# Planner steps per scan and delayed TensorE sums in the last chunks of an attention and Mamba kernel

## The chip, the cores and the metric

The kernel runs on one core of one Trainium2 chip. The time is that of the device, in microseconds (us), the median of several executions. The engines are named as in the profile: PE is TensorE (PEld its weight loads), DVE is VectorE, ACT is ScalarE, POOL is GpSimd, and SP issues the loads and stores of this kernel. Each engine works through its own queue in the order in which the program issued it.

## What is computed

Two layers follow each other, on four images of 128 channels and 64 x 64 pixels, in f32. The first is attention over the 4096 pixels of an image (four heads of 32), with an output projection, a residual and a layer norm. The second is the sum of three things: a 3 x 3 convolution, a spectral part (a 1 x 1 convolution on the Fourier transform), and a Mamba block. Only the last matters here:

```python
xi, z = split(in_proj(u))                  # 256 inner channels each
xs = silu(causal_conv1d(xi, 4 taps))
dt, Bm, Cm = split(x_proj(xs))             # dt through dt_proj and softplus
h[n]  = exp(dt * A[n]) * h[n] + dt * Bm[n] * xs      # 16 states n, along the pixels
y     = sum over n of h[n] * Cm[n], + xs * D
out   = out_proj(y * silu(z))
```

## The kernel before

The pixels are cut into 32 chunks of 512 (eight per image). A chunk's 256 inner channels are two halves of 128 partitions, so a chunk has 2 x 16 = 32 states, each a row of work on 128 x 512 elements:

- ACT computes the decay `dA = exp(dt * A)` into PSUM (`scan_decay`, L813), for which there are two PSUM tiles in the tail.
- DVE in the tail, POOL before it, computes the input term `db = u * B` (`scan_input_term`, L818).
- DVE runs the recurrence (`scan_state`, L829), called the scan of a state below.
- POOL copies the last column into `state` (L838, left out in the last chunk of an image) and multiplies by C in place (L839).
- The product is added to the chunk's sum: by POOL into an SBUF tile (L856 and L858) for all chunks but the last two. For chunks 30 and 31 it is added by PE, with an identity matrix as weights, into a PSUM tile (L851 for the first term, L852 for the states). There the scan writes into one of four tiles of V that attention no longer needs.

B and C of a state pair are broadcast from DRAM to all partitions by two rows of a load on SP (L796 into one of three ring buffers, L802 into tiles of K or V that attention has left, which the list `spare` hands out). A state pair needs 512 KB.

One Python loop writes all instructions out in a fixed order; nothing is reordered afterwards. Its counter t advances by one for each block of keys of the attention (32 blocks, 64 chunk and head-pair combinations: t from 0 to 2047) and runs on to 2239. A chunk's states take 64 steps, one state on every even step; the scan of chunk c begins at step 144 + 64 c. So when attention ends, chunk 29 still has its states 24 to 31 to scan, and chunks 30 and 31 come after it, at steps 2064 and 2128. This last part, from t = 2049, is called the tail. On an even step the loop issues the scan, the copy, the multiplication and the addition of a state; on an odd step the decay of the next state, the input term of the one after it, and a load.

Everything else is written as generators, "jobs", that a `Plan` advances: the projections, the layer norm, the input of the next chunk's scan (`mamba_input`, `scan_input`, `scan_bc`, `scan_dt`), `spectral`, `convolve` (nine taps and a tenth matmul, L903 and L908), the gate `silu(z)` of a chunk (`gate`), `scan_output` (gate, out_proj, sum), and `flips` (the last sum of the chunks whose mirrored rows come late). A job yields what its next piece needs: "P", "D" and "A" are places on PE, DVE and ACT, "B" is one of two PSUM banks, "f" the right to the one output tile, and an empty string only the next step. `plan.step` is called once in every t and gives each job, in order of rank, at most one advance if there are places left; only PE pieces may follow each other in the same call. In the tail each call has four places of each of the three engines. `sigmoid`, used by the gate and by `scan_input`, yields five such pieces: ACT abs (L615), ACT exp (L617), ACT ln into a bank (L620), DVE combination (L623), ACT exp (L625).

Between the scan of a state and the next in DVE's queue stand the input term and whatever jobs have put there; between two decays on ACT, likewise; between the additions of two states on PE, likewise. In `scan_state` the addition on PE is issued right after POOL's multiplication, in the same step.

Of the kernel before, what the change touches and what calls it, by code (L numbers as in the profile page):

```python
# [9 lines left out]
F32 = mybir.dt.float32  # L10
F32R = mybir.dt.float32r
AF = mybir.ActivationFunctionType
ALU = mybir.AluOpType
# [4 lines left out]
P = 128  # L18
# [5 lines left out]
L = 512  # L24
# [3 lines left out]
NH = DI // P  # L28
NS = 16
# [52 lines left out]
class Job:  # L82
# [4 lines left out]
    def __init__(self, gen):  # L87
        self.gen = gen
        self.done = False
        self.need = None  # L90
        self.advance(None)
# [8 lines left out]
class Plan:  # L100


    def __init__(self, banks, buffers):
        self.t = None
        self.places = buffers
        self.seq = 0
        self.later = []
        self.jobs = []
        self.free = list(range(banks))
        self.freed = []  # L110
# [11 lines left out]
    def step(self, t, places):  # L122

        self.t = t
        self.places |= places
        self.free += [bank for when, bank in self.freed if when <= t]
        self.freed = [e for e in self.freed if e[0] > t]
        for e in sorted((e for e in self.later if e[0] <= t), key=lambda e: e[:3]):
            self.jobs.append((e[1], e[0], e[2], Job(e[3])))
            self.later.remove(e)  # L130
        self.jobs = sorted((j for j in self.jobs if not j[3].done), key=lambda j: j[:3])
        kept = 0
        for *_, job in self.jobs:
            bank = None
            if "B" in job.need and len(self.free) <= kept:
                continue
            if any(c != "B" and not self.places[c] for c in job.need):
                kept += "B" in job.need
                continue
            for c in job.need:  # L140
                if c == "B":
                    bank = self.free.pop(0)
                else:
                    self.places[c] -= 1
            job.advance(bank)
            while not job.done and job.need == "P" and self.places["P"]:
                self.places["P"] -= 1
                job.advance(None)
        self.jobs = [j for j in self.jobs if not j[3].done]

# [5 lines left out]
def attention_then_conv_mamba(  # L156
# [17 lines left out]
    nc = tc.nc  # L174
# [3 lines left out]
    NT = N // P  # L178
    CHUNKS = B * NCH
    HALVES = CHUNKS * PAIRS  # L180
# [4 lines left out]
    loc = ctx.enter_context(tc.tile_pool(name="loc", bufs=2))  # L185
    dram = ctx.enter_context(tc.tile_pool(name="dram", bufs=2, space=DRAM))
    psum = ctx.enter_context(tc.tile_pool(name="psum", bufs=1, space=PSUM))
# [12 lines left out]
    for h in range(HEADS):  # L200
        k, j = divmod(h, 2)
        c = COL["bk"] + k
# [8 lines left out]
    for h in range(HEADS):  # L211
        k, j = divmod(h, 2)
        c = COL["bq"] + h
# [33 lines left out]
    ident = cst[:, K_ID : K_ID + P]  # L247
# [64 lines left out]
    plan = Plan(2, {"x": 2, "f": 1})  # L312
# [315 lines left out]
    xps, xss, dts, us, accs, gates, xds, bcds = ({} for _ in range(8))  # L628
# [154 lines left out]
    spare = [((HALVES - 1) * NT + 1, KK[0][i : i + 2]) for i in range(0, NCH, 2)]  # L783
    spare += [(HALVES * NT + 12, KK[1][i : i + 2]) for i in range(0, NCH, 2)]
    spare += [(HALVES * NT + 20, VA[i : i + 2]) for i in range(4, NCH, 2)]
    taken, ring = {}, [3]
# [33 lines left out]
    def scan_state(c, v):  # L820

        n, hf = divmod(v, NH)
        k = hf * NS + n
        assert (c, hf) in scaled
        if c >= CHUNKS - 2:
            hs = flat(VA[v % 4])
        else:
            hs = loc.tile([P, L], F32, tag="hs", name=f"hs_{c}_{k}")
        nc.vector.tensor_tensor_scan(  # L829
            hs,  # L830
            dA.pop((c, v)),
            db.pop((c, v)),
            state[:, k : k + 1] if c % NCH else zero,
            ALU.mult,
            ALU.add,
        )
        if c % NCH < NCH - 1:
            nc.gpsimd.tensor_copy(state[:, k : k + 1], hs[:, L - 1 :])  # L838
        nc.gpsimd.tensor_tensor(hs, hs, bcs[c, n][1], ALU.mult)  # L839
        if hf == NH - 1 and (c, n) in taken:  # L840
            spare.append((plan.t + 6, taken.pop((c, n))))
        elif hf == NH - 1:
            ring[0] += 1
        if c >= CHUNKS - 2:

            if v == 0:
                late = psum.tile([P, NH, L], F32, tag=f"s{CHUNKS - c}", name=f"acc_{c}")
                for h in range(NH):
                    accs[c, h] = late[:, h, :]
            if n == 0:  # L850
                nc.tensor.matmul(accs[c, hf], ident, xss[c][hf], start=True, stop=False)  # L851
            nc.tensor.matmul(accs[c, hf], ident, hs, start=False, stop=n == NS - 1)  # L852
        elif n == 0:
            acc = loc.tile([P, L], F32, tag=f"acc{hf}", name=f"acc_{c}_{hf}")
            accs[c, hf] = acc
            nc.gpsimd.tensor_tensor(acc, xss[c][hf], hs, ALU.add)  # L856
        else:
            nc.gpsimd.tensor_tensor(accs[c, hf], accs[c, hf], hs, ALU.add)  # L858

    hxs, yms, edges, wd, ymd = {}, {}, set(), {}, {}  # L860

# [74 lines left out]
    def scan_output(c):  # L936

        b, i = divmod(c, NCH)
        late = i < NCH // 2
        yield "f"  # L940
        while not all(gates[c]) or c not in yms:
            yield ""

        for hf in range(NH):
            if c >= CHUNKS - 2:
                acc = loc.tile([P, L], F32, tag=f"acc{hf}", name=f"acc_{c}_{hf}")
                nc.vector.tensor_tensor(acc, accs[c, hf], gates[c][hf], ALU.mult)
                accs[c, hf] = acc
            else:
                nc.gpsimd.tensor_tensor(accs[c, hf], accs[c, hf], gates[c][hf], ALU.mult)  # L950
        if not late:
            wr = load_flipped(c)
        for _ in range(3):
            yield ""
        bank = yield "PB"
        pf = bank_tile(bank, [P, L], f"py1_{c}")
        for hf in range(NH):
            if hf:
                yield "P"
            nc.tensor.matmul(  # L960
                pf, outw[:, hf, :], accs[c, hf], start=hf == 0, stop=hf == NH - 1
            )
        yield "D"
        plan.release(bank, 2)
        ob = loc.tile([P, L], F32, tag="ob", name=f"ob_{c}", bufs=1)
        nc.vector.tensor_tensor(ob, yms.pop(c), pf, ALU.add)
        if late:
            yield ""
            ymd[c] = dram.tile([P, L], F32, tag="ymd", name=f"ymd_{c}", bufs=NCH)
            nc.sync.dma_start(ymd[c], ob)  # L970
        else:
            add_flipped(ob, wr)
            yield ""
            yield ""
            nc.sync.dma_start(out[b, :, i * L : (i + 1) * L], ob)
        plan.places["f"] += 1
# [20 lines left out]
    LEAD = 7  # L997
    SLOT = PAIRS * NT
    LAG = 2 * SLOT + 16
# [19 lines left out]
    for c in range(CHUNKS):  # L1019
        t0 = (c + 1) * SLOT  # L1020
        plan.at(t0, 0, load_residual(c))
        plan.at(t0 + 16, 1, mamba_input(c))
        plan.at(t0 + SLOT + 30, 3, convolve(c))
        plan.at(c * SLOT + LAG + 6, 3, gate(c))
        plan.at((c + 1) * SLOT + LAG + 2, 0, scan_output(c))
    for b in range(B):
        for i in range(NCH // 2):
            plan.at((b + 1) * NCH * SLOT + 44 + 10 * i, 4, flips(b * NCH + NCH // 2 - 1 - i))
# [1 line left out]
    t = 6 - SLOT  # L1030
    loaded = 0
    end = (CHUNKS + 3) * SLOT
    while t < end or not plan.idle():
        H, m = divmod(t, NT)
        if 0 <= H < HALVES:
            scores_for_exp(H, m)
        h1, s1 = divmod(t + LEAD, NT)
        if 0 <= h1 + 1 < HALVES:
            scores_for_max(h1 + 1, s1)
        H, m = divmod(t - 1, NT)  # L1040
        last = m == NT - 1
        if last and 0 <= H < HALVES:
            times_values(H, m)
        c, s = divmod(t - LAG, SLOT)
        odd = s % 2 == 1
        if -1 <= c < CHUNKS:
            v = c * STATES + s // 2
            if not odd:
                if v >= 0:
                    scan_state(*divmod(v, STATES))  # L1050
            else:
                if 0 <= v + 1 < CHUNKS * STATES:
                    scan_decay(*divmod(v + 1, STATES))
                if 0 <= v + 2 < CHUNKS * STATES:
                    late = t > HALVES * NT
                    scan_input_term(
                        *divmod(v + 2, STATES), nc.vector if late else nc.gpsimd
                    )

                if loaded < CHUNKS * NS and loaded // NS in bcds:  # L1060
                    if ring[0] or spare[0][0] <= t:
                        scan_load(*divmod(loaded, NS))
                        loaded += 1
        if t < -LEAD or t > HALVES * NT:
            plan.step(t, {"D": 4, "P": 4, "A": 4})
        elif odd:
            plan.step(t, {"D": 2, "P": 2, "A": 2})
        else:
            plan.step(t, {"D": 0, "P": 0, "A": 1})
        if not last and 0 <= H < HALVES:  # L1070
            times_values(H, m)
        t += 1
# [76 lines left out]
```

## Time and profile before

| | us |
|---|---|
| median of 3 runs | 6135.8 (6135.27 to 6138.95) |
| the profiled execution, its own time | 6136.61 |
| its span | 6134.7 |
| attention's last matmul ends about | 5891 |
| scan of state 0 of chunk 30 starts | 5923.6 |
| scan of state 0 of chunk 31 starts | 6042.7 |
| last scan starts | 6122.8 |

Over the whole span PE is busy for 5914.9 us (96%), DVE for 4291.6, ACT for 3557.2 and POOL for 4534.8. These are averages over a long attention stage and a short tail; the tail has to be read for itself. In the tables of stretches a line gives start and end, length, and then the busy time of each engine with its number of instructions. In the order of time a line gives start, duration, engine, source line, operation, output and inputs, and in brackets how long the engine stood idle before it and what ended the wait. In the list of waits a line gives who waited for whom, the total, the number of times and the longest. In names, V and K are attention's tiles, in the tail used for the scan's results and for B and C.

### The profile page before, as it was taken

How to read it: one execution, taken by the hardware profiler on the slowest of the kernel's cores; microseconds unless marked ns; L12 is line 12 of the kernel's file. 1: busy time of each engine (PE TensorE's matmuls, PEld its weight loads, DVE VectorE, ACT ScalarE, POOL GpSimd, SP SyncE). 2: the span in 40 equal slices, each digit the busy share in tenths (PEclk: the TensorE clock that was granted, in tenths of full speed). 3: DMA queues.
4: the chain of work that ended last, by engine and by line, in shares of the span. 5: the costliest groups of instructions: out<-in, count | busy, mean ns of one | idle time of the engine just before them, and what ended most of it. 6: DMA issues, size and time to landing. Idle time of an engine off the chain costs nothing. (4 is left out here: it accounts for less than half of the span.)

```text
span 6134.7 us, 82692 instructions
## 1 busy us (share of the span) xinstructions
PE 5914.9 (96%) x31434; PEld 2454.4 (40%) x31434; DVE 4291.6 (70%) x4404; ACT 3557.2 (58%) x4794; POOL 4534.8 (74%) x4785
## 2 busy tenths in 40 slices
PE   5999999999999999999999999999999999999966
PEld 2444444444444444444444444444444444444321
DVE  4556776777776777777767777677777677777647
ACT  1455666665666665666665666666565566566643
POOL 0006888778887777888877888877888787788877
PEclk7999999999999999999999999999999999999988
DMA  4012222224322222222332322222432222222222
GB/s 126 23 35 57 75 65 73 72 69 110 89 78 74 72 70 71 73 66 84 102 89 72 74 75 65 73 72 68 111 82 75 69 65 63 65 66 69 67 82 82
DMA packets 265503, 455.21 MB, mean 74 GB/s; under 512 B 45577, under 2 KB 47121, under 8 KB 265105
## 3 DMA queue, kind: packets, MB, share of 16 engines
q1 hardware_dynamic: 261584, 448.11, 26.9%
q8 instruction: 246, 4.03, 0.3%
q10 hardware_dynamic: 3520, 1.82, 0.1%
q14 instruction: 153, 1.25, 0.1%
HBM read 375.63 MB, written 65.80 MB: 72 GB/s over the span
## 5 line engine op out<-in xcount | busy, mean ns | idle before, releaser
L446 DVE TENSOR_REDUCE part<-s 128x2 f32<-128x1024 f32 x2048 | 2497.4, 1220 | 1527.0 <-PE s L439 1526.5
L491 ACT ACTIVATE e<-s 128x1024 f32<-128x1024 f32 x2048 | 2095.3, 1023 | 2203.1 <-PE s L483 2195.7
L503 PE MATMUL po<-e,V 128*33 128x512 f32 x8192 | 2158.6, 605 | 0.7
L483 PE MATMUL s<-Q,K 64*128 64x512 f32 x8192 | 1504.0, 445 | 7.1 <-ACT e L491 3.8
L439 PE MATMUL s<-K,Q 64*128 64x512 f32 x8192 | 1314.6, 398 | 31.5 <-DVE part L446 28.5
L839 POOL TENSOR_TENSOR hs<-hs,bc 128x512 f32<-128x512 f32 x952 | 1215.7, 1277 | 174.0 <-DVE hs L829 105.4
L483 PEld LDWEIGHTS s<-Q,K 64*128 64x128 f32 x8192 | 610.9, 185 | 1727.9 <-ACT e L491 1175.1
L818 POOL TENSOR_TENSOR db<-u,bc 128x512 f32<-128x512 f32 x948 | 1215.4, 1282 | 0.0
L858 POOL TENSOR_TENSOR acc<-acc,hs 128x512 f32<-128x512 f32 x900 | 1150.8, 1279 | 70.6
L829 DVE TENSOR_TENSOR_SCAN hs<-dA,state,db 128x512 f32<-128x512 f32 x832 | 1060.2, 1274 | 106.9 <-ACT dA L813 53.1
L439 PEld LDWEIGHTS s<-K,Q 64*128 64x128 f32 x8192 | 762.0, 185 | 255.2 <-DVE part L446 77.1
L483 PE MATMUL s<-MX,sel 64*128 64x512 f32 x4096 | 813.4, 394 | 25.9 <-DVE MX L470 25.9
L813 ACT ACTIVATE dA<-dt,negA 128x512 f32<-128x512 f32 x1024 | 703.1, 687 | 137.3 <-DVE hs L829 76.1
L838 POOL COPY state<-hs 128x1 f32<-128x1 f32 x864 | 159.9, 185 | 818.1 <-DVE hs L829 818.1
L503 PEld LDWEIGHTS po<-e,V 128*33 128x33 f32 x8192 | 299.8, 109 | 908.4 <-issue 894.1
L483 PEld LDWEIGHTS s<-MX,sel 64*128 64x128 f32 x4096 | 384.0, 184 | 129.2 <-DVE MX L470 38.6
L903 PE MATMUL pf<-xp,cw 128*128 128x512 f32 x576 | 288.5, 620 | 0.0
L455 POOL COPY wide<-mx 128x128 f32<-128x128 f32 x256 | 63.1, 290 | 202.5 <-DVE mx L452 202.5
L829 DVE TENSOR_TENSOR_SCAN hs<-dA,zero,db 128x512 f32<-128x512 f32 x128 | 163.0, 1274 | 1.5 <-POOL db L818 1.2
L852 PE MATMUL acc<-V,cst 128*128 128x512 f32 x128 | 92.4, 823 | 71.6 <-POOL V L839 71.2
L903 PEld LDWEIGHTS pf<-xp,cw 128*128 128x128 f32 x576 | 96.7, 188 | 135.4 <-issue 135.2
L701 POOL TENSOR_TENSOR xs<-xs,sg_x 128x512 f32<-128x512 f32 x64 | 82.4, 1287 | 59.1 <-ACT sg_x L625 59.1
(141 smaller groups left out, 3551.4 us busy)
## 6 DMA issues: line engine op xcount, KB each, us to landing
bc<-bcd SPq DMA_DIRECT2D x487, 512.0 KB
Q<-qd SPq DMA_DIRECT2D x256, 128.0 KB
K<-kd SPq DMA_DIRECT2D x64, 256.0 KB
K<-bcd SPq DMA_DIRECT2D x42, 256.0 KB
vd<-vst SPq DMA_DIRECT2D x32, 264.0 KB
V<-vd SPq DMA_DIRECT2D x32, 264.0 KB
xq<-in_x SPq DMA_DIRECT2D x32, 256.0 KB
xk<-in_x SPq DMA_DIRECT2D x32, 256.0 KB
```

The costliest lines, as they stand in the source:

```text
L439: nc.tensor.matmul(sc[:, j, :], QT[H][rows[j], n, t * P : (t + 1) * P], KK[k][m][rows[j], :], start=n == 0, stop=n == 1,)
L446: nc.vector.tensor_reduce(part[H][:, t, :, m], sc, AX.X, ALU.max)
L483: nc.tensor.matmul(s[:, j, :], sel[rows[j], :] if n == 2 else KK[k][i][rows[j], t * P : (t + 1) * P], mov[rows[j], :], start=n == 0, stop= ...
L491: nc.scalar.activation(e, s, AF.Exp)
L503: nc.tensor.matmul(po[H][used[j], :], VA[i][:, t, 2 * k + j, :], e[:, j, :], start=m == 0, stop=m == NT - 1,)
L813: nc.scalar.activation(dA[c, v], dts[c][hf], AF.Exp, scale=negA[:, k : k + 1])
L818: engine.tensor_tensor(db[c, v], us[c][hf], bcs[c, n][0], ALU.mult)
L829: nc.vector.tensor_tensor_scan(hs, dA.pop((c, v)), db.pop((c, v)), state[:, k : k + 1] if c % NCH else zero, ALU.mult, ALU.add,)
L838: nc.gpsimd.tensor_copy(state[:, k : k + 1], hs[:, L - 1 :])
L839: nc.gpsimd.tensor_tensor(hs, hs, bcs[c, n][1], ALU.mult)
L858: nc.gpsimd.tensor_tensor(accs[c, hf], accs[c, hf], hs, ALU.add)
L903: nc.tensor.matmul(pf, cw[:, k, :], xps[c][:, dy : dy + RPC, dx : dx + W], start=k == 0, stop=False)
```

## The change

In the tail (`plan.late`), four things differ.

- `plan.step` is called on odd steps only, so once for each scan and not twice, with four places on DVE and PE and six on ACT. Within one call a job now advances over as many "P", "A" and "D" pieces as follow each other, while there are places. It stops at an empty yield, at a bank, and at a need for two things at once.
- The addition of a state on PE is not issued with its scan, but kept in a list and issued two scans (four steps) later (`add_states`).
- From step 2052 on, the states of chunk 29 (26 to 31) are also summed by PE; its first 26 states stay in POOL's sum. `scan_output` then adds the two sums on DVE (two more instructions), and chunk 29's gate is multiplied on DVE and no longer on POOL.
- `scan_output` of chunks 29 to 31 becomes due four steps later. The test for a free load buffer also holds when `spare` is empty.

```diff
--- before.py
+++ after.py
@@ -102,6 +102,7 @@
 
     def __init__(self, banks, buffers):
         self.t = None
+        self.late = False
         self.places = buffers
         self.seq = 0
         self.later = []
@@ -143,8 +144,11 @@
                 else:
                     self.places[c] -= 1
             job.advance(bank)
-            while not job.done and job.need == "P" and self.places["P"]:
-                self.places["P"] -= 1
+
+            while not job.done and job.need in ("PAD" if self.late else "P"):
+                if not job.need or not self.places[job.need]:
+                    break
+                self.places[job.need] -= 1
                 job.advance(None)
         self.jobs = [j for j in self.jobs if not j[3].done]
 
@@ -822,7 +826,8 @@
         n, hf = divmod(v, NH)
         k = hf * NS + n
         assert (c, hf) in scaled
-        if c >= CHUNKS - 2:
+        late = plan.t > HALVES * NT + 1
+        if late:
             hs = flat(VA[v % 4])
         else:
             hs = loc.tile([P, L], F32, tag="hs", name=f"hs_{c}_{k}")
@@ -841,21 +846,31 @@
             spare.append((plan.t + 6, taken.pop((c, n))))
         elif hf == NH - 1:
             ring[0] += 1
-        if c >= CHUNKS - 2:
-
-            if v == 0:
-                late = psum.tile([P, NH, L], F32, tag=f"s{CHUNKS - c}", name=f"acc_{c}")
-                for h in range(NH):
-                    accs[c, h] = late[:, h, :]
-            if n == 0:
-                nc.tensor.matmul(accs[c, hf], ident, xss[c][hf], start=True, stop=False)
-            nc.tensor.matmul(accs[c, hf], ident, hs, start=False, stop=n == NS - 1)
+        if late:
+
+            if c not in sums_late:
+                sums_late[c] = psum.tile(
+                    [P, NH, L], F32, tag=f"s{1 + c % 2}", name=f"acc_{c}"
+                )
+            terms = [hs] if n else [xss[c][hf], hs]
+            for x in terms:
+                waiting.append((plan.t + 4, c, hf, x, n == NS - 1 and x is hs))
         elif n == 0:
             acc = loc.tile([P, L], F32, tag=f"acc{hf}", name=f"acc_{c}_{hf}")
             accs[c, hf] = acc
             nc.gpsimd.tensor_tensor(acc, xss[c][hf], hs, ALU.add)
         else:
             nc.gpsimd.tensor_tensor(accs[c, hf], accs[c, hf], hs, ALU.add)
+
+    sums_late, waiting, begun = {}, [], set()
+
+    def add_states():
+        while waiting and waiting[0][0] <= plan.t:
+            _, c, hf, x, last = waiting.pop(0)
+            nc.tensor.matmul(
+                sums_late[c][:, hf, :], ident, x, start=(c, hf) not in begun, stop=last
+            )
+            begun.add((c, hf))
 
     hxs, yms, edges, wd, ymd = {}, {}, set(), {}, {}
 
@@ -942,10 +957,14 @@
             yield ""
 
         for hf in range(NH):
-            if c >= CHUNKS - 2:
-                acc = loc.tile([P, L], F32, tag=f"acc{hf}", name=f"acc_{c}_{hf}")
-                nc.vector.tensor_tensor(acc, accs[c, hf], gates[c][hf], ALU.mult)
-                accs[c, hf] = acc
+            if c in sums_late:
+                total = sums_late[c][:, hf, :]
+                if (c, hf) in accs:
+                    nc.vector.tensor_tensor(accs[c, hf], accs[c, hf], total, ALU.add)
+                    total = accs[c, hf]
+                else:
+                    accs[c, hf] = loc.tile([P, L], F32, tag=f"acc{hf}", name=f"acc_{c}_{hf}")
+                nc.vector.tensor_tensor(accs[c, hf], total, gates[c][hf], ALU.mult)
             else:
                 nc.gpsimd.tensor_tensor(accs[c, hf], accs[c, hf], gates[c][hf], ALU.mult)
         if not late:
@@ -1022,7 +1041,7 @@
         plan.at(t0 + 16, 1, mamba_input(c))
         plan.at(t0 + SLOT + 30, 3, convolve(c))
         plan.at(c * SLOT + LAG + 6, 3, gate(c))
-        plan.at((c + 1) * SLOT + LAG + 2, 0, scan_output(c))
+        plan.at((c + 1) * SLOT + LAG + (2 if c < CHUNKS - 3 else 6), 0, scan_output(c))
     for b in range(B):
         for i in range(NCH // 2):
             plan.at((b + 1) * NCH * SLOT + 44 + 10 * i, 4, flips(b * NCH + NCH // 2 - 1 - i))
@@ -1058,10 +1077,16 @@
                     )
 
                 if loaded < CHUNKS * NS and loaded // NS in bcds:
-                    if ring[0] or spare[0][0] <= t:
+                    if ring[0] or spare and spare[0][0] <= t:
                         scan_load(*divmod(loaded, NS))
                         loaded += 1
-        if t < -LEAD or t > HALVES * NT:
+        plan.late = t > HALVES * NT
+        if plan.late:
+            add_states()
+            if odd:
+                plan.step(t, {"D": 4, "P": 4, "A": 6})
+            plan.t = t
+        elif t < -LEAD:
             plan.step(t, {"D": 4, "P": 4, "A": 4})
         elif odd:
             plan.step(t, {"D": 2, "P": 2, "A": 2})
```

## The prediction

> **What bounds the kernel now.** I read the page first, then busy time by stretches, the waits of the tail and the order of time. `plan.late` is only set for t > 2048, so before that step the edited planner issues the same instructions; attention ends at 5891 us and only what follows can move.
>
> The stretches of the profile before, from the end of attention to scan 0 of chunk 30, to scan 0 of chunk 31, to the last scan's end, to the end (length, then busy time of each engine, granted clock, DMA share, GB/s):
>
> ```profile
> 5891.00:5923.60 32.60, 5.33 (x10) 1.75 (x8) 21.69 (x30) 12.73 (x22) 31.18 (x30) 0.58 0.18 48
> 5923.60:6042.70 119.10, 73.64 (x119) 26.11 (x120) 81.63 (x84) 45.42 (x80) 79.31 (x91) 0.74 0.48 139
> 6042.70:6124.10 81.40, 56.29 (x96) 17.71 (x94) 64.38 (x68) 26.83 (x42) 59.39 (x39) 0.87 0.15 46
> 6124.10:6134.70 10.60, 4.21 (x8) 1.27 (x8) 1.97 (x3) 0.00 (x0) 2.78 (x4) 1.00 0.07 25
> ```
>
> No engine fills the last two chunks: DVE is busy 146 of 200 us. Before that, POOL is (31.2 of 32.6). Undisturbed, a state costs this much (order of time, late in chunk 31):
>
> ```profile
> 6092.20 0.69 DVE L818 TENSOR_TENSOR db<-u,V 128x512 f32<-128x512 f32 x1
> 6092.24 1.77 POOL L839 TENSOR_TENSOR V<-V,bc 128x512 f32<-128x512 f32 x1 [0.15 <-DVE V L829]
> 6092.81 1.28 DVE L829 TENSOR_TENSOR_SCAN V<-dA,state,db 128x512 f32<-128x512 f32 x1
> ...
> 6094.12 0.69 DVE L818 TENSOR_TENSOR db<-u,V 128x512 f32<-128x512 f32 x1
> ```
>
> Scan and product repeat every 1.92 us: 64 states need 123 us of DVE alone, and take 200. The waits of the tail (total, times, longest):
>
> ```profile
> PE acc L852 <- POOL V L839: 71.2, 39, 6.0
> ACT dA L813 <- DVE V L829: 57.4, 39, 6.1
> ...
> DVE V L829 <- ACT dA L813: 20.8, 9, 5.6
> ACT zg L775 <- PE pz L769: 14.4, 4, 6.8
> DVE ob L966 <- PE py L960: 12.7, 3, 7.1
> ```
>
> PE stands on its additions (L852) until POOL has multiplied, so what jobs put behind them is late; ACT then waits for these matmuls with the next decays behind it, and DVE for the decays. The longest knot, in order of time:
>
> ```profile
> 5977.74 7.03 PE L903 MATMUL pf<-xp,cw 128*128 128x512 f32 x16
> ...
> 5985.56 1.12 PE L726 MATMUL pdt<-xd,dtw 8*128 8x512 f32 x2
> ...
> 5986.71 0.69 ACT L734 ACTIVATE dt<-pdt,vec 128x512 f32<-128x512 f32 x1 [7.48 <-PE pdt L726]
> ...
> 5989.73 0.68 ACT L620 ACTIVATE ln_z<-sg_z,ones 128x512 f32<-128x512 f32 x1
> ...
> 5990.45 0.69 DVE L623 SCALAR_TENSOR_TENSOR sg_z<-zg,ln_z 128x512 f32<-128x512 f32 x1 [8.37 <-ACT ln_z L620]
> 5991.06 1.28 DVE L829 TENSOR_TENSOR_SCAN V<-dA,state,db 128x512 f32<-128x512 f32 x1
> ```
>
> **What the skill says.** The Trainium skill, "SBUF — State Buffer", Who interferes with whom: a DVE instruction with two SBUF inputs shuts out a GpSimd instruction that reads SBUF, and the reverse, for a whole instruction. The trace agrees: the product (u and bc in SBUF, 0.69) makes POOL's multiplication 1.77 instead of 1.26 when they start together, and is itself 1.5 to 1.8 where POOL came first; the scan, with dA in PSUM, stays at 1.27. "TensorE: Matmul & The Clock Gate", What's actually happening: the array runs at half clock after idle windows and at full clock after busy ones. An addition (two matmul records) takes 2.08 after an idle stretch and 1.02 in a busy one, here.
>
> **The change part by part.** I followed the planner's rules by hand through both orders and reckoned each engine's queue with the durations above; ACT operations count 0.6 each, POOL tensor operations 1.26 plus 0.2 for the state's copy, DVE ones 0.6 start to start.
>
> *From 2049 to chunk 30 (before: scan 30.0 at 5923.6).* Taken away: POOL's additions for the last six states of chunk 29, six by 1.41 (L858's mean here) = 8.5. PE takes them, idle otherwise, two scans later. Added: one step now sends ACT zg, abs and exp, the next ln, and DVE's combination waits for ln ahead of scan 29.26. ACT has ten operations from 5893.6 (6.3 us), so this scan starts at 5900.6 instead of 5898.2: 2.4 lost. Then POOL: gate product 5902.6, a multiplication 4.8, three operations of dt with two products in their way 9.9, four multiplications 17.0, op*rz 18.3. The projection pa needs op*rz, takes 2.08 cold, and DVE's xr waits for it ahead of scan 30.0, in the same step now: about 5921. Gain 2.6. On SP, the zc load now stands behind a ring load that waits for multiplication 29.25; it moves from 5893.8 to about 5900, rz to 5911.7, and op*rz, which POOL reaches at 5917, covers that; uncovered it would cost up to 3.
>
> *Chunk 30, scans 0 to 8 (before 36.5, to 5960.1).* Eight pitches of 1.92 = 15.4; bn 1.3, four DVE operations for chunk 29 (two sums read from PSUM, two gates; not seen before, L947's 0.68 each is nearest; 0.6 to 1.3 each with a lock) 2.8, xh 1.3, two gate combinations 1.2, ob 0.6; waits for ACT 1.2, lock 1.2. Sum 24.9, to 5945.9: gain 14.2 so far. The gain is the 7.1 before ob (py1 now runs between additions that wait for nothing) and the 3.9 before the convolution by taps.
>
> *Scans 8 to 14 (before 31.0).* Six pitches 11.5; eight tap operations 5.4; two combinations 1.3; waits for ln 2.8 (tap operations, abs, exp, ln and combination follow each other); lock 1.1. Sum 22.1, to 5968: 23 so far.
>
> *Scans 14 to 19 (before 19.9).* Five pitches 9.6, dt twice 1.2. PE: pw ends 5964, four convolution taps, addition, pd, three taps, addition, three: 13.8 us at 0.87 a tap, to 5977.8. ACT's xd waits for pd and then ym for the last tap, in the step that issues it, the next decays behind: 2.4 and 5.0 on DVE. Then six dt activations ahead of a decay: 3.0. Sum 21.2: 5989.4; the knot stays and costs what it did. 21.6 so far.
>
> *Scan 19 to chunk 31 (before 31.7).* Here POOL is next: dt's six operations (8.2), twelve multiplications at 1.46 plus 0.6 for each product's lock, three flips at 1.9. A scan writes the tile of four states ago, so it waits for that addition, and that for POOL. POOL is busy without a break from 5987 until about 6030; scan 31.0 comes at 6023, 33.6 after. 19.7 so far. The load of ob is now issued two scans ahead of the flip, so POOL's 3.6 for it is gone.
>
> *Chunk 31, scans 0 to 11 (before 42.4).* Eleven pitches 21.1; chunk 30's gates and ob 1.9, combinations 1.2; POOL's lag at the start 1 to 2; pz behind addition 31.1, then zg, abs, exp, decay, ln, combination: 4; the convolution's end (k0 at 6046, hil at 6057) holds ym and decay 11: 5. Sum 35.3, to 6058.3: 26.8 so far. From there 20 states at 1.9 and 10.6 of end, unchanged.
>
> Total 26, allowing 1 for hand-offs: span 6134.7 − 26 = 6108.7, that execution's own time 6136.6 − 26 = 6110.6. The median of the runs, 6135.8, is 0.8 below its own time: 6110.
>
> **Rivals.** (1) *The ACT chains wait less than I reckon*, since engines run ahead. Without the waits and locks of the stages from chunk 30 on (2.4 + 3.9 + 10.4 + 10), 27 more would go: 6083, and 6075 to 6098 as its range. For it: DVE holds 1.92 wherever jobs rest. Against: abs to combination is data dependence. (2) *The wait moves, nothing comes of it*: seven combinations now stand ahead of a scan in the step that sends their ln, and POOL's lag takes what PE's had. I count about 2 each; at 5 the seven take 21 of the 26: about 6131. For it: the 8.4 above was such a combination. Against: most were within 1 us in the run before. (3) *Slower: the convolutions on a half clock.* PE, no longer fed in one burst of eight taps, may run cold. Each tap then takes 2.08 rather than 0.87: 12 for ten taps, 3 for the additions between, and pi, pd, pw, pdt, py1 and pz about 9 in all, all ahead of an evacuation with a decay behind it: 2 by 15 + 9 = 39, giving 6149. It decides once two thirds of this holds. For it: the clock of 0.58 to 0.74 in the stretches above. Against: chunk 30's burst is at 0.88 a tap. (4) *A load is late*: nine loads of 512 KB follow each other one a scan in chunk 30; at 1.92 us each that asks for more than the 139 GB/s moved there, but each is four scans ahead of its use and no wait of DVE for a load shows. That belongs to (2).
>
> **How the numbers follow.** Forecast (6098 to 6122) 0.55; rival 1 0.13; 2 and 4 (6122 to 6148) 0.20; 3 0.12. Of 6135.8, 0.2% is 12.3 us, about what a measurement can tell. Faster holds the forecast, rival 1 and the edge of 2: 0.70; same 0.18; slower 0.12. The range leaves out a tenth on each side: 6092, within rival 1, and 6140, within 2; the unseen DVE operations (2.4 to 5.2 in all) lie well inside.
>
> **What would show it.** Right: PE's wait of 71.2 for POOL's products shrinks to a fraction of itself or has no job's matmul behind it; the 7.1 before ob goes; scan 30.0 near 5921, 31.0 near 6023, the last near 6096; POOL without idle before chunk 31. Wrong: DVE waiting for ACT's ln or decay by more than 3 at each combination (rival 2); convolution taps at 2 us (rival 3); DVE waiting for PE's additions over all of chunk 30, when POOL would be the bound much earlier than I have it.

## The result, and the profile after

The changed kernel takes 6114.2 us (median of 6 runs, 6110.9 to 6116.5) against 6136.4 (6134.1 to 6139.0) for the kernel before: a ratio of 0.9963, 95% interval 0.995 to 0.9975. The forecast was 6110, 6092 to 6140.

The stretches of the profile after, cut at the same events as before: end of attention, scan 0 of chunk 30, scan 0 of chunk 31, end of the last scan, end (length, busy time of PE, PEld, DVE, ACT and POOL, granted clock, DMA share, GB/s):

```profile
5891.60:5920.00 28.40, 10.20 (x14) 2.68 (x12) 21.03 (x21) 13.62 (x23) 26.75 (x26) 0.64 0.20 57
5920.00:6029.10 109.10, 70.51 (x127) 25.46 (x127) 84.35 (x97) 45.88 (x79) 77.28 (x87) 0.75 0.52 152
6029.10:6101.30 72.20, 52.75 (x97) 17.23 (x95) 64.67 (x68) 26.91 (x41) 60.48 (x39) 0.93 0.18 51
6101.30:6111.90 10.60, 4.23 (x8) 1.27 (x8) 1.98 (x3) 0.00 (x0) 2.78 (x4) 0.98 0.07 25
```

The three stretches of the tail shrink from 32.6, 119.1 and 81.4 to 28.4, 109.1 and 72.2, and the end stays at 10.6. DVE is busy for 172.0 us of the four stretches, 169.7 before, so what went is idle time of DVE. In the names below, pa is the output projection of attention, pz the matmul of a gate, pd and pdt those of x_proj and dt_proj, pf the convolution (its taps), ym its copy by ACT, and py1 the out_proj behind the output tile ob. The waits of the tail after, from the list:

```profile
ACT dA L817 <- DVE V L834: 66.9, 42, 5.9
PE acc L870 <- POOL V L844: 65.0, 36, 13.0
...
DVE V L834 <- ACT dA L817: 17.2, 5, 5.1
...
DVE V L834 <- PE acc L870: 7.1, 2, 3.8
...
DVE sg_z L627 <- ACT ln_z L624: 4.9, 4, 2.7
```

PE still waits 65.0 us for POOL's products (71.2 before), but the two totals don't cover the same additions. The first waits after are those of chunk 29's additions, which PE did not have before (order of time, PE):

```profile
5905.01 2.08 PE L870 MATMUL acc<-V,cst 128*128 128x512 f32 x2 [12.96 <-POOL V L844]
5911.19 5.88 PE L870 MATMUL acc<-V,cst 128*128 128x512 f32 x6 [4.09 <-POOL V L844]
```

They make up 17.1 of the 65.0; for chunks 30 and 31 the wait went from 71.2 to 48. Waits for what stands behind an addition went too. The 12.7 of ob waiting for py1 are down to 1.9, and instead of 8.4 before one combination there are six waits of 2.7 at most, 7.7 in all (sg_x, not shown, has 2.8 in two). The decays (17.2 after, 20.8 before) still come late, and at the place that was forecast. Chunk 30's convolution, in order of time, from the answers for PE, ACT and DVE:

```profile
5968.09 3.60 PE L918 MATMUL pf<-xp,cw 128*128 128x512 f32 x8
...
5972.48 1.91 PE L716 MATMUL pd<-xs,xpw 128*40 128x512 f32 x4
5974.32 2.84 PE L918 MATMUL pf<-xp,cw 128*128 128x512 f32 x6
...
5974.42 0.59 ACT L720 ACTIVATE xd<-pd 40x512 f32<-40x512 f32 x1 [6.00 <-PE pd L716]
...
5975.63 1.28 DVE L834 TENSOR_TENSOR_SCAN V<-dA,state,db 128x512 f32<-128x512 f32 x1 [3.84 <-ACT dA L817]
...
5980.63 0.69 ACT L928 ACTIVATE ym<-pf,vec 128x512 f32<-128x512 f32 x1 [5.04 <-PE pf L923]
...
5981.93 1.28 DVE L834 TENSOR_TENSOR_SCAN V<-dA,state,db 128x512 f32<-128x512 f32 x1 [4.30 <-ACT dA L817]
```

ACT stands on pd, which stands behind four taps that were issued in a burst, and then on the last tap; each time the decay behind it is late for DVE. Four taps take 3.6 us, 0.9 each: the array is warm here.

### The profile page after: what moved, and what is told of

It reads as the page before. It is cut to its first block, busy times and chain, and to the rows that moved or that the text cites. A ratio compares the mean times of both kernels' runs of the same rounds, so it can differ in the third digit from the quotient of the medians.

```text
span 6111.9 us, 82705 instructions
## 1 busy us (share of the span) xinstructions
PE 5917.5 (97%) x31446; PEld 2452.4 (40%) x31446; DVE 4296.0 (70%) x4408; ACT 3561.5 (58%) x4794; POOL 4535.9 (74%) x4777
## 5 line engine op out<-in xcount | busy, mean ns | idle before, releaser
L834 DVE TENSOR_TENSOR_SCAN hs<-dA,state,db 128x512 f32<-128x512 f32 x826 | 1053.5, 1275 | 98.8 <-ACT dA L817 48.3
L443 PEld LDWEIGHTS s<-K,Q 64*128 64x128 f32 x8192 | 762.0, 186 | 257.5 <-DVE part L450 81.4
```

The source lines that it names most:

```text
L443: nc.tensor.matmul(sc[:, j, :], QT[H][rows[j], n, t * P : (t + 1) * P], KK[k][m][rows[j], :], start=n == 0, stop=n == 1,)
L834: nc.vector.tensor_tensor_scan(hs, dA.pop((c, v)), db.pop((c, v)), state[:, k : k + 1] if c % NCH else zero, ALU.mult, ALU.add,)
```

## Experiments

The change has three parts that can be had apart: the new steps of the planner (S), the delay of PE's additions (D), and chunk 29's sums on PE (C). The experiments first take their combinations, then look into D, S and what remains. Beside the median I use the *tail*: in the profile, from the start of the scan of state 24 of chunk 29 (written 29.24), the last that the change leaves where it was, to the end. It leaves out what attention's 5890 us vary by (29.24 starts between 5889 and 5895 in these profiles). All kernels but the one before keep the fourth part, the later due time of the last outputs. A kernel with that due time and none of S, D and C was not run.

| kernel | parts | median us | ratio to before (95%) | tail us | scan 30.0, 31.0 after 29.24 |
|---|---|---|---|---|---|
| before | none, old due time | 6136 to 6138 | 1 | 242.4 | 31.4, 150.5 |
| the change | S D C | 6114.2 | 0.9963 (0.995 to 0.9975) | 219.0 | 27.2, 136.2 |
| e1 | S C | 6158.1 | 1.0033 (1.002 to 1.0046) | 265.5 | 31.1, 165.8 |
| e2 | D C | 6103.6 | 0.9945 (0.993 to 0.996) | 211.9 | 28.0, 132.1 |
| e3 | S D | 6120.3 | 0.9971 (0.996 to 0.9982) | 226.8 | 34.4, 144.1 |
| e4 | S | 6160.2 | 1.0038 (1.0024 to 1.0052) | 269.1 | 34.4, 169.1 |
| e5 | D | 6111.0 | 0.9958 (0.9941 to 0.9974) | 215.9 | 31.4, 133.5 |
| e12 | C | 6149.1 | 1.0019 (1.0012 to 1.0026) | 257.0 | 36.3, 162.6 |

The due time changes the order of the jobs in chunk 30. Before, pd runs ahead of the convolution's taps. In e4 and e12, which have the due time in common but none of S, D and C, it runs behind four and behind seven of them (order of time, PE; before, e4, e12; a tap is two records):

```profile
5974.47 1.91 PE L712 MATMUL pd<-xs,xpw 128*40 128x512 f32 x4
5977.74 7.03 PE L903 MATMUL pf<-xp,cw 128*128 128x512 f32 x16
```

```profile
6001.78 4.73 PE L918 MATMUL pf<-xp,cw 128*128 128x512 f32 x8
6007.29 1.91 PE L716 MATMUL pd<-xs,xpw 128*40 128x512 f32 x4
```

```profile
5982.49 2.95 PE L918 MATMUL pf<-xp,cw 128*128 128x512 f32 x6
5986.14 3.60 PE L918 MATMUL pf<-xp,cw 128*128 128x512 f32 x8
5989.67 1.91 PE L716 MATMUL pd<-xs,xpw 128*40 128x512 f32 x4
```

So two kernels that both have the later due time show what a part is worth, while e4, e5 and e12 against the kernel before show a part and the due time together. Only up to scan 30.0, at step 2064, do they show the part alone: the earliest of these outputs was due at step 2066.

**e1: without the delay.** The addition goes out with its scan again:

```diff
-                waiting.append((plan.t + 4, c, hf, x, n == NS - 1 and x is hs))
+                waiting.append((plan.t, c, hf, x, n == NS - 1 and x is hs))
```

> The changed kernel with PE's addition issued in the step of its scan, as before, instead of two scans later; planner and third last chunk as changed. Measured by the tail, from the start of scan 29.24 to the end: 242.4 us before, 219.0 with the change. Theory M (the delay frees the jobs' matmuls from POOL): the 7.1 before ob and the 3.9 before the taps of chunk 31 come back, and more at pz and pd; tail 230 to 242. Theory N (the planner's steps do it, the delay is idle): tail 216 to 222.

The tail is 265.5: theory N is out, and so is the size that theory M gave. The delay is worth 46.5 here, more than the whole gain; without it the rest of the change, due time included, loses 23. PE's wait for POOL's products is 110.5 in e1 and 65.0 with the delay.

**e2: the old steps, with delay and chunk 29.**

```diff
-            if odd:
-                plan.step(t, {"D": 4, "P": 4, "A": 6})
-            plan.t = t
+            plan.step(t, {"D": 4, "P": 4, "A": 4})
...
-            while not job.done and job.need in ("PAD" if self.late else "P"):
+            while not job.done and job.need in "P":
```

> The changed kernel with the planner's old steps in the tail (a call in every t, four places each, one advance, only PE pieces chained); delay and third last chunk as changed. Theory M: most of the gain stays, tail 217 to 228, and the waits that the chains inside one step cause (ln before the combination, 1 to 2.7 each) get shorter. Theory N: the gain goes, tail 238 to 244.

The tail is 211.9, below theory M's range and 7.1 less than with the new steps, and no combination waits for ln any more. So the new steps are a loss that the gain of the delay covers. DVE's longest waits in e2, as the list has them:

```profile
DVE V L834 <- ACT dA L817: 18.5, 6, 9.5
DVE V L834 <- PE acc L870: 4.0, 2, 3.8
DVE xr L569 <- PE pa L566: 3.9, 1, 3.9
```

**e3: chunk 29 on POOL.**

```diff
-        late = plan.t > HALVES * NT + 1
+        late = c >= CHUNKS - 2
```

> The changed kernel with the last six states of chunk 29 summed by POOL again, as before; delay and planner as changed. Both theories: POOL's 8.5 come back in the stretch that POOL fills, two DVE sums (1.3) go and two products go back to POOL (2.9); scan 30.0 comes 3 to 8 later than 27.2 after scan 29.24, tail 221 to 226. If chunk 29 carried most of the gain: tail above 230.

Tail 226.8, 0.8 past the range: chunk 29's part is worth 7.8 beside the other two. Scan 30.0 comes 7.2 later (34.4 instead of 27.2) and the rest of the tail keeps that.

**e4: of the three parts, the new steps alone** (the edits of e1 and e3).

> The kernel before with the new steps of the planner alone (additions in the step of their scan, chunk 29 on POOL; the later due time of the last outputs is kept). Theory M: near the kernel before, tail 236 to 248. Theory N: tail 220 to 228.

Neither theory had this: 269.1, 26.7 worse than before. By scan 30.0, before the due time can act, 3.0 are lost (34.4 against 31.4). What the rest is of the steps and what of the due time, the runs do not part. e1 against e12, which share everything but the steps and have no delay either, puts the steps at 8.5. The list of DVE's waits in e4 begins:

```profile
DVE sg_z L627 <- ACT ln_z L624: 25.1, 5, 7.6
DVE V L834 <- ACT dA L817: 23.2, 4, 7.8
DVE ob L985 <- PE py L979: 14.0, 3, 6.4
```

and one of the five combinations, in order of time, shows how a chain sent in one call holds DVE:

```profile
5956.88 2.08 PE L870 MATMUL acc<-V,cst 128*128 128x512 f32 x2 [6.21 <-POOL V L844]
...
5958.75 1.91 PE L773 MATMUL pz<-xp,inw 128*128 128x512 f32 x2
...
5960.76 0.60 ACT L779 ACTIVATE zg<-pz 128x512 f32<-128x512 f32 x1 [6.63 <-PE pz L773]
...
5964.24 0.67 ACT L624 ACTIVATE ln_z<-sg_z,ones 128x512 f32<-128x512 f32 x1
...
5965.01 0.69 DVE L627 SCALAR_TENSOR_TENSOR sg_z<-zg,ln_z 128x512 f32<-128x512 f32 x1 [7.63 <-ACT ln_z L624]
```

The matmul, its copy, abs and exp go out in one call, ln and combination in the next. pz stands behind an addition that waits 6.2 for POOL; ACT stands on pz; DVE stands on ln with the next scan behind the combination; and POOL gets nothing to multiply until that scan has run. With the old steps these pieces are spread over six calls, with scans between them.

**e5: of the three parts, the delay alone** (the edits of e2 and e3).

> The kernel before with the addition on PE two scans later alone (old steps, chunk 29 on POOL; the later due time of the last outputs is kept). If the delay carries the gain and the parts add up: the third last chunk was worth 7.8 of tail beside the new steps (226.8 against 219.0), so the tail is 211.9 + 3 to 9 = 215 to 221, against 242.4 before. If delay and third last chunk need each other: 230 or more.

Tail 215.9: the delay and the later due time together give 26.5, more than the whole change (23.4). Up to scan 30.0 nothing has moved (31.4 in both), since chunk 29's sums are on POOL here.

**e12: of the three parts, chunk 29 alone** (the edits of e1 and e2).

> The kernel before with the last six states of chunk 29 summed by PE, alone (old steps, additions in the step of their scan; the later due time of the last outputs is kept). With the other parts present it was worth 3.6 to 7.8 of tail; if the parts add up, the tail is 242.4 - 4 = 236 to 240. If PE's additions of chunk 29, waiting for a POOL that is behind, hold the projection and the layer norm of chunk 31: 242 or more.

257.0: with the later due time it loses 14.6. Its additions wait for a POOL that is behind, and pa and py of the projection stand behind them:

```profile
5906.44 3.78 PE L870 MATMUL acc<-V,cst 128*128 128x512 f32 x4 [16.08 <-POOL V L844]
...
5919.11 0.75 DVE L569 SCALAR_TENSOR_TENSOR xr<-pa,bo,xr 128x512 f32<-128x512 f32 x1 [7.81 <-PE pa L566]
...
5926.18 0.89 DVE L580 BATCH_NORM_STATS2 st<-py 128x6 f32<-128x128 f32 x4 [4.40 <-PE py L573]
```

By scan 30.0 that has cost 4.9 (36.3 against 31.4), and this is chunk 29's part alone. The remaining 9.7 come later in the tail, where this kernel differs from the one before by the later start of chunk 31's input and the later due time of the outputs; I did not part these two.

Between kernels that both have the due time, the parts nearly add up. The delay is worth 42.3 with S, 45.1 with C and 46.5 with both. S costs 7.1 and 10.9 with the delay, and 8.5 without it. C gives 4.0 and 7.8 with the delay, and 3.6 without it beside S. C does change its sign at scan 30.0: by itself it brings that scan 4.9 later, with the delay 3.4 earlier, with S 3.3 earlier.

The missing kernel can be estimated from these. In the three pairs what C is worth at the end is what it was worth at scan 30.0, within 0.7; e12 without its 4.9 would end at 252. e5 without a delay worth 42 to 46, or e4 without steps that cost 7 to 11, would end at 258 to 262. By this estimate the due time costs 10 to 20 of the tail and the delay is worth 36 to 47 by itself, and the change holds a loss that none of these runs took out. That is not shown: no run has the due time alone, or the delay with the old one.

**e7: a delay of one scan** (e2, and):

```diff
-                waiting.append((plan.t + 4, c, hf, x, n == NS - 1 and x is hs))
+                waiting.append((plan.t + 2, c, hf, x, n == NS - 1 and x is hs))
```

> The kernel of the old steps with delay, with the addition one scan later instead of two. POOL's multiplication ends about 1.3 to 1.9 after its scan, and a scan takes 1.92, so where POOL is not behind one scan of delay should do: tail 212 to 217 if only the ordinary lag has to be covered. If POOL's backlog of several operations is what held PE: 220 to 235.

218.9 (median 6114.0), between the two ranges: one scan gives 38 of the 45 that two give over e12, and PE's wait is 101.2, 75.3 and 62.2 with no delay, one scan and two. Most of what held PE was POOL's ordinary lag, and the second scan takes some of the backlog.

**e6: chains in every call** (the call of e2 with the advance of the change: only the first hunk of e2's edit).

> The kernel of the old steps with delay, but a job advances over as many P, A and D pieces as follow each other in one call; a call still comes in every t with four places each. It parts the new steps' loss of 7.1 (219.0 against 211.9) into the chains and the rarer calls. If the chains cost it (the combination stands in DVE's queue ahead of the scan while ACT still does abs, exp and ln): DVE waits for ACT's ln come back, 5 or more in all, tail 217 to 224. If the rarer calls cost it: tail 209 to 214 and no waits for ln over 1 in all.

228.0 (median 6120.8), beyond the range on the side of the chains. They cost 16.1 over e2, and DVE waits 13.3 for ln_z in five combinations again (none in e2). The rarer calls of the change give 9.0 of that back. New steps without the chains weren't run: chunk 31's dt would not be issued before its first scan.

**e8: ten tiles for the scans' results** (e2, and):

```diff
-            hs = flat(VA[v % 4])
+            if not late_hs:
+                late_hs.extend(flat(VA[j]) for j in range(4))
+                for j in range(3):
+                    et = att.tile([P, 2, L], F32, tag="e", name=f"late_hs_{j}", bufs=3)
+                    late_hs.extend(et[:, r, :] for r in range(2))
+            hs = late_hs[(c * STATES + v) % len(late_hs)]
```

> The kernel of the old steps with delay, with ten tiles for the scans' results instead of four (attention's three e tiles give six more). The scan's waits for PE's addition (6.6 of DVE in the kernel without this) are waits for such a tile: they go. If POOL and DVE then only run with more slack: tail 205 to 209. If POOL is the bound in the second half of chunk 30, the scan runs ahead and waits for something else, and the tail stays at 210 to 213.

The scans no longer wait for an addition, scan 31.0 comes 5.6 earlier, and by scan 31.11 nothing is left of it (162.0 after 29.24, against 162.3). The tail is 211.6, the median 6105.1. Chunk 30's gate now waits 2.8 for the sums and a decay 3.0. The four tiles are where POOL's backlog shows, not its cause.

**e9, e10, e11: the convolution.** All on e2, for chunks 30 and 31. e9 issues ym three scans after the last tap:

```diff
+        if c >= CHUNKS - 2:
+            for _ in range(6):
+                yield ""
         yield "A"
```

> The kernel of the old steps with delay; ACT's copy of the convolution's result (ym) of chunks 30 and 31 comes three scans after the last tap instead of in the next call. It asks how much of DVE's longest wait for a decay (9.5, in chunk 30) and of that in chunk 31 (2.4) is ACT standing on the last tap. ACT waited 5.3 for pd and 1.7 for the last tap before that decay. If the last tap alone holds it: 9.5 falls by no more than 1.7, 2.4 goes, tail 208 to 210. If the wait only moves to pd: tail 210 to 213.

e10 issues two taps a call:

```diff
         for k in range(9):
+            if k and k % 2 == 0 and c >= CHUNKS - 2:
+                yield ""
             if k:
                 yield "P"
```

> The kernel of the old steps with delay; the convolution of chunks 30 and 31 issues two taps a call instead of four, so pd finds fewer taps ahead of it on PE. If the taps ahead of pd are the knot: the 9.5 falls to 5 or less, tail 205 to 209. If ACT then waits for the last tap as long: tail 210 to 213.

e11 does both, with one tap a call (k % 1).

> Both: one tap a call, and ym three scans after the last tap. If PE's burst of taps is the whole of the knot, 9.5 and 2.4 go: tail 200 to 204. If another wait takes the place (dt's six activations, POOL's three operations for dt, or pdt): tail 206 to 211.

The tails are 207.0, 207.1 and 205.1, the medians 6099.9, 6101.3 and 6098.8. e11 is 0.9938 of the kernel before (0.9923 to 0.9953), the fastest here by the tail; the ratios of e2 and these three can't be told apart. e9 is below both of its ranges, e10 within that for the taps, and e11 between its two. In e2 the scan behind the knot, and in e11 the waits that are left there (order of time, DVE, first e2, then e11):

```profile
5970.86 1.28 DVE L834 TENSOR_TENSOR_SCAN V<-dA,state,db 128x512 f32<-128x512 f32 x1 [9.53 <-ACT dA L817]
```

```profile
5968.18 1.28 DVE L834 TENSOR_TENSOR_SCAN V<-dA,state,db 128x512 f32<-128x512 f32 x1 [1.76 <-ACT dA L817]
...
5976.54 1.28 DVE L834 TENSOR_TENSOR_SCAN V<-dA,state,db 128x512 f32<-128x512 f32 x1 [1.07 <-ACT dA L817]
...
5981.68 1.28 DVE L834 TENSOR_TENSOR_SCAN V<-dA,state,db 128x512 f32<-128x512 f32 x1 [2.92 <-ACT dA L817]
```

At this place the waits for decays are 9.5 in e2, 6.1 in e9, and 1.8, 2.4 and 0.7 in e10. So the burst of taps ahead of pd was the larger part of the knot, and ACT standing on the last tap a smaller one, though more than the 1.7 expected. Of 6.8 that e11 gained by scan 30.14 (75.0 after 29.24, against 81.8) 3.6 are left at scan 30.19 (91.9 against 95.5), since pdt and dt's activations are then late, and 3.3 at 31.0 (128.8 against 132.1). Chunk 31 adds the rest.

## Why the prediction held, and where it did not

By the points at which the prediction cut the tail, in us after scan 29.24:

| | before | predicted | measured |
|---|---|---|---|
| scan 30.0 | 31.4 | 28.7 | 27.2 |
| scan 30.8 | 67.8 | 53.6 | 53.2 |
| scan 30.14 | 98.8 | 75.7 | 76.9 |
| scan 30.19 | 118.7 | 97.1 | 100.1 |
| scan 31.0 | 150.5 | 130.7 | 136.2 |
| scan 31.11 | 192.9 | 166.0 | 169.4 |
| end | 242.4 | 216.4 | 219.0 |

*Up to scan 30.0: right, a little low.* The combination before scan 29.26 waits 2.7 for ln, and that scan starts 8.1 after 29.24, where 8.3 was reckoned. xr waits 3.8 for pa as foreseen; pa takes 1.12 and not 2.08, and that is most of the difference. That chunk 29's additions have warmed the array for it is likely, not shown: pa takes 2.07 or 2.08 in the kernels without these additions on PE, and anything from 1.02 to 1.92 in those with them.

*Scans 0 to 8: right* (26.0 for 24.9). This stage gives the largest part of the gain, 10.4 of 23.4, and e1 shows that it is the delay's: without it the stage takes 45.6. That additions would wait for nothing was too much said: PE still waits 28.5 for them in chunk 30.

*Scans 8 to 19: right in kind* (23.7 and 23.2 for 22.1 and 21.2). The knot stayed, as the step said: the three waits for decays are 3.8, 4.3 and 3.3, 11.5 for the reckoned 10.4; pw ran cold (2.07 and 1.91).

*Scan 19 to chunk 31: the step that failed.* It took 36.1, not 33.6, the largest miss of a stage. "POOL's 3.6 for it is gone" was wrong: POOL waits 3.4 for wr. The order of issue is as I had it, but SP had stood in front of it: first on a load whose V tile POOL had not yet left, then on a ring load, and then 3.8 on the store of the flip before, which has to leave the one ob tile. From POOL's and SP's order of time in the profile after:

```profile
5992.35 11.46 SPq L806 DMA_DIRECT2D V<-bcd  x2
6011.67 0.37 SPq L800 DMA_DIRECT2D bc<-bcd  x1
6012.13 0.42 SPq L1009 DMA_DIRECT2D out<-ob  x1
...
6017.43 0.32 SPq L1002 DMA_DIRECT2D ob<-ymd  x1
6017.79 0.43 SPq L939 DMA_DIRECT2D wr<-wd  x1
...
6020.88 1.25 POOL L948 TENSOR_TENSOR ob<-ob,wr 128x504 f32<-128x504 f32 x1 [3.44 <-DMA wr<-wd]
```

I had counted how many scans ahead the load was issued, and not whom SP waits for before it: for POOL, the very engine that is behind, and for the store that POOL's last flip released.

*Chunk 31: better than reckoned* (33.2 for 35.3). The two combinations wait 0.7 and 0.15, where I had put 4 on pz and its chain; the convolution costs 5.1, as said.

*Luck in the sum.* The sum is right to 3 us, but not every stage is: by the table four stages were reckoned 7.0 too short in all and three 4.4 too long. (The 21.2 after 5968 leads to 5989.2; the prediction went on from 5989.4.)

*What the prediction did not see.* It added the gain of the delay and the cost of the chains stage by stage, but never asked for each part by itself. e2 against the change, and e5 against e3, show that the new steps belong to the losses. It followed the new order in the queues without asking what the due time alone does to it. The waits for ln that I allowed (2.4, 1.2, 2.8 and most of 4) come to about 10; 7.7 are measured, and 7.1 is what e2 saves. Of the sign "PE's wait of 71.2 shrinks to a fraction of itself or has no job's matmul behind it" the first half did not come: of the 71.2, 48 are left for the same two chunks.

*The rivals.* The first, less waiting in the chains, was not this kernel; e2, which has no chains, gains 7.1 more, not the 27 of that rival. The second, the chains eat the gain, is right about the place and wrong about the size as long as the delay is there: about 1 each, not 5. In e4, without the delay, the gates' five wait 5 each. The third, cold convolutions, falls: 0.9 us a tap. The late loads of B and C of the fourth did not show as waits of DVE; the load that was late is wr's, for POOL, by 3.4.

## What to carry to other kernels

An instruction that waits for another engine holds what is queued behind it. Issuing PE's additions later took 42.3 to 46.5 us off the tail in three pairs of kernels, and 39.0 to 45.5 off PE's own wait (92.8 to 51.5 in e4 and e3, 101.2 to 62.2 in e12 and e2, 110.5 to 65.0 in e1 and the change). Issue the consumer of another engine's product some steps later in an in-order queue: here one scan gave 38 and two gave 45, and more was not tried. When two totals of a wait are compared, see that they cover the same instructions.

Keep the pieces of a dependent chain over several engines apart, with the pacing work between them. Sent whole in one call, the chains cost 16.1 here (e6 against e2), and DVE waited 13.3 for their ln where it had waited for none.

Where a change has several parts, cost each part with the others there and with the others gone, and let each control differ in one thing only. Here a due time went along with every part and was never run by itself, so that a part against the kernel before says less than it seems to.

## What the runs showed that I had not expected

The part that looked safe, POOL's adds moved to an idle PE, by itself brings scan 30.0 4.9 us later; with the delay, or with the new steps, it brings it 3.4 or 3.3 earlier. And PE's clock differs with the stalls: in chunk 31 the granted clock is 0.87 before and 0.93 after, and about the same work keeps PE busy for 56.3 and 52.8 us. So some of the shorter matmuls are probably a consequence of the waits that went.
